# Another order of the steps between two expert layers, and a weight load issued behind the loop instead of in it

## The chip, the cores and the metric

The kernel runs on one core of a Trainium2 chip. Its engines are TensorE (PE: matmuls; PEld is its weight load, which overlaps), VectorE (DVE), ScalarE (ACT), GpSimd (POOL) and SyncE (SP). Each runs its own instructions in program order and waits for the others by semaphores; DMA transfers are issued from an engine's queue (here SP's, ACT's and POOL's) and move by themselves. The metric is the time of one execution on the device in microseconds (us); the lower the better.

## What is computed

Two layers on x, (4, 512, 512) f32 (2048 tokens of width 512), each an attention part and an expert part, gated by the tanh of a scalar:

```python
x = x + tanh(g_xattn[0]) * set_attention(layernorm(x), ctx)     # every token, 4 sets of 64
x = x + tanh(g_ffn[0])   * experts0(layernorm(x))               # 32 experts, top 6, at most 192 tokens each, + shared expert
x = x + tanh(g_xattn[1]) * causal_mha(layernorm(x), ctx, ctx)   # 16 heads, 64 keys
x = x + tanh(g_ffn[1])   * experts1(layernorm(x))               # 8 experts, top 2, inner width 352, + shared expert
```

Two facts of the reference matter for what follows. In the second attention the mask hides all 64 keys from every token but the last 64 of a batch; those others get the plain mean of the values, so the kernel computes that attention for the last row tile of each batch alone. And the shared expert of the last layer, `silu(x Wg + bg) * (x Wu + bu) Wd + bd` with inner width 704, needs no routing: it is computed in two halves (inner widths 320 and 384), the first of them between the two expert loops.

## The kernel before

**Tiles.** The 2048 tokens are 16 row tiles of 128 rows, x0 to x15, resident in SBUF. Tile t belongs to batch t // 4; a group g holds the tiles g, 4+g, 8+g, 12+g, one of each batch, so that group 3 has the last tile of every batch: 3, 7, 11, 15.

**The first expert loop** runs over pieces of experts, PE-bound, and writes weighted rows to y_dram. A token's sum over its experts is formed by fetches: one POOL indirect DMA (L1063) fetches, for one row tile, the k-th expert's row of each of its 128 tokens into a buffer `yk` (7 buffers, NYK), and one DVE addition puts it on the tile (L1104; L1106 for a tile's last one, which also leaves the row sums for the layer norm; then one ACT Square, L1057, gives the sum of squares). There are 76 fetches in all (six for tiles 0 to 8, fewer for the others). The string SUMS (L68) gives their order; the first 22 are asked for while the loop still runs, the other 54 behind it. At L1258 stands a branch on a count of tokens (not taken here), which every engine passes; POOL waits there for its outstanding fetches. I number the sums whose fetch is issued behind it s1 to s54; in front of s1 stand six more whose fetches were issued before it.

**The stage between the loops** is written out by hand. The string ORDER (L49) is a list of step names; in_steps (L671) calls them one after the other, and each call issues the next part of a generator. The engines' program order is exactly the order in which the parts issue. The steps:

- `s` (sums4): one addition (and Square), then the request for the next fetch.
- `e2`, `e3` (shared0): the first layer's shared expert on groups 2 and 3: two chunks of gate and up products on PE (L630, 16 matmul records each), Silu on ACT (L636), two DVE instructions that give `it0s` (L642, L643), then per tile the output product (PE L650, in one of two PSUM buffers `po0s`) and its addition on DVE (L657).
- `q` (query3): layer norm of group 3 on ACT (L1274), after a reciprocal root on DVE (L1121 and helpers). `a0`, `a1` (stage3): the attention for two batches each: transposes `ptq`, scores, softmax, output; it ends with additions on group 3's tiles and new Squares.
- `n0` to `n3` (norm4), `t0` to `t3` (turn_in4), `l0` to `l3` (logs): layer norm of a group (ACT L1133), its transposes (PE L282, ACT L283), the router's logits (PE L1146, L1152) and the choice of two experts (DVE L1159 to L1168).
- `d0` to `d3` (shared4): the first half of the last layer's shared expert on a group: PE L1361 (gate, up), ACT L1366, DVE L1367, PE L1377 and L1384, DVE L1387. Its weights are those that `k` loads first.
- `r0`, `r1` (route4): for half of the tokens (groups 0 and 1; then 3 and 2): positions on PE (L1175, L1176), some 40 DVE instructions that end with the table `ent` (L1209 to L1211), then 16 POOL indirect DMAs (L1216) that scatter the entries to slot_dram.
- `p` (plan4): a plan of expert tiles on DVE from the totals (PE L1419), then the request of the finished slot table from DRAM (POOL L1460, `tab`), a selection by matmul (PE L1464, `pslot`), and from it on DVE the row numbers `gat` and `put` by which the last expert loop gathers and scatters.
- `w` (first_weights): POOL gathers of two expert tiles' weights (L1396).
- `k` (loads): first call, on ACT's queue, load_shared4: gate and up weights (L782, 1.31 MB) and down weights (L783, 0.52 MB; L786, twice 0.13 MB) of the last layer's shared half; second call the keys and values of two batches (L1245, L1246, 1.5 MB).

Steps that stand in the ORDER ahead of PE's or ACT's arrival at the branch's far side may in the built program lie beside the loop's end on that engine: before, `k`'s first call is issued by ACT at 427 to 437 us, in the loop's last two pieces.

**Behind the stage**, from 641.6 us on, the last expert loop and the second half of the shared expert run, on PE almost without a gap.

```python
    while coming:          # sums4
        add4()
        ask4(NT2 - 1)
        yield
```

Of the kernel before, what the change touches and what calls it, by code (L numbers as in the profile page):

```python
# [46 lines left out]


ORDER = """  # L49
e3 s k s*2 e3*2 s*4 e3 e2 s*7 e2 s*2 e3 s*2 e3 s*2 e3 s*2 e3 s*4 e2 s e2 s q e2 n0 e2*2 n0 s*4 a0 a1 s*2 n0 t0  # L50
a0 n0 s n0 t0 s t0*2 a0 s e2 s*3 k s*3 l0 s d0 n1 d0 n1 s d0*2 n1 t1 l0 d0 l0 n1*2 a0 t1 s*2 d0 s t1 s a1 t1 a0
l1 s a1 a0 s*2 d1 s a1 l1*2 d0*2 a1 s*2 d1 a1 r0 s*2 n3*2 s n3 d1 r0 n3 s t3 s d1 t3 n3 n2 d0 r0 n2*3 r0 t3 r0
t3 n2 d1 d0 t2*2 l3 t2*2 d3 d1 d3 l2 r0 l3 l2 r0 l3 r0 l2 d1 r1 r0 d2 r1 p r1*3 d1 p d3 d2 r1 d1 d2 d3 d2*2 d1
r1 p r1 d2 p d2 d3 r1 d2 w p d3*2 p d3 p*2 w d3*2 d2 p d2
"""


# [8 lines left out]

NAHEAD = 22
SUMS = """  # L68
3 7 0 4 8 3 7 0 4 8 3 7 0 4 8 3 7 0 4 8 6 2 3 4 8 7 8 4 12 0 11 12 11 12 0 7 15 1 15 11 3 1 5 1 9 5 9 1 9 1 9 5
5 13 13 13 1 5 9 5 6 14 2 10 6 2 2 14 10 6 6 6 10 2 2 10  # L70
"""
NW = 3
NW0 = 4
# [1671 lines left out]
```

## Time and profile before

| | us |
|---|---|
| median of 3 runs | 1056.91 (1056.79 to 1057.18) |
| the profiled execution | 1056.65 |
| its span | 1054.9 |
| PE busy in it | 982.4 (93%) |
| DVE, POOL, ACT busy | 445.9, 380.5, 196.1 |
| the stage between the loops | 437.6 to 641.6 |

Times in the profile count from the span's start. An instruction's row in a timeline reads: start, duration, engine, line, operation, out<-in, tile sizes, how many were merged (x8), and in brackets the time its engine sat idle before it and what released it. A line "A <- B: 7.6, 1, 7.6" in the list of waits gives total, number and longest.

A few rows of waits in the stage (437 to 642 us):

```profile
POOL yk L1063 <- DVE x L1104: 16.7, 10, 5.7
DVE x L1104 <- DMA yk<-y_dram,rows_of: 11.8, 15, 2.6
PE po0s L650 <- DVE x L657: 7.6, 1, 7.6
DVE x L1106 <- DMA yk<-y_dram,rows_of: 6.3, 9, 2.2
PE po0s L650 <- DVE it0s L643: 3.2, 1, 3.2
DVE it L1367 <- ACT sg L1366: 3.0, 3, 1.9
```

and the loads of the shared half's weights on ACT's queue:

```profile
427.09 0.39 ACTq L782 DMA_DIRECT2D wall<-in_wsgu1a_dram  x1
429.69 0.49 ACT L870 ACTIVATE sgb<-g 128x384 f32<-128x384 f32 x1 [3.73 <-PE g L865]
435.87 0.39 ACTq L783 DMA_DIRECT2D wall<-in_wsd_dram  x1
436.29 1.17 ACTq L786 DMA_DIRECT2D wall<-in_wsd_dram  x2
```

### The profile page before, as it was taken

The page shows a single profiled execution, that of the slowest core. Times are in us where ns is not written, and L with a number is a line of the kernel's source. Part 1 is how long each engine was busy: PE and PEld are TensorE (multiplying, and loading weights), DVE is VectorE, ACT ScalarE, POOL GpSimd, SP SyncE. Part 2 cuts the span into 40 slices and gives each one's busy share as a digit, 9 for nine tenths or more (in the row PEclk, how much of TensorE's full clock was granted, in tenths as well). Part 3 has the DMA queues.
Part 4 walks back from the last instruction along what each step waited for, and adds up shares of the span by engine and source line. Part 5 has one row for each costly group of instructions (what it writes and reads, how often), then busy time and mean ns, then how long its engine had stood idle before and what let it go on. Part 6 is the DMA issues. An engine that isn't in the chain of part 4 may idle for free. (4 is left out here: it accounts for less than half of the span.)

```text
span 1054.9 us, 11755 instructions
## 1 busy us (share of the span) xinstructions
PE 982.4 (93%) x3762; PEld 578.3 (55%) x3762; DVE 445.9 (42%) x1218; ACT 196.1 (19%) x410; POOL 380.5 (36%) x420
## 2 busy tenths in 40 slices
PE   5568889999999999978999979999999999999998
PEld 2133348777878787634554434555555555544443
DVE  4878973323222322568885442122222222227111
ACT  1263111111111111015544002111111111100000
POOL 3001053353333333767623634445545445200000
PEclk8889989999999999989999989999999999999999
DMA  8722135798888799957722066247536535537111
GB/s 316 307 101 80 45 92 175 235 306 284 264 312 280 283 321 336 339 161 212 249 77 91 1 169 204 79 140 235 168 95 197 163 103 171 193 122 255 40 40 40
DMA packets 88671, 192.03 MB, mean 182 GB/s; under 512 B 24910, under 2 KB 42222, under 8 KB 82208
## 3 DMA queue, kind: packets, MB, share of 16 engines
q1 hardware_dynamic: 58800, 110.82, 29.4%
q0 software_dynamic: 28656, 76.76, 24.1%
q10 hardware_dynamic: 1152, 3.67, 1.0%
q8 instruction: 31, 0.51, 0.2%
q14 instruction: 32, 0.26, 0.1%
HBM read 206.16 MB, written 35.60 MB: 229 GB/s over the span
## 5 line engine op out<-in xcount | busy, mean ns | idle before, releaser
L1063 POOL DMA_INDIRECT yk<-y_dram,rows_of x76 | 84.4, 1111 | 50.4 <-DVE x L1104 18.4
L834 POOL DMA_INDIRECT xb<-h_dram,get x48 | 48.0, 1000 | 145.5 <-DVE get L830 71.0
L1586 PE MATMUL por<-wall,itr 128*128 128x512 f32 (+1 forms) x216 | 98.7, 592 | 0.0
L865 PEld LDWEIGHTS g<-lnT,wall 128*128 128x128 f32 x512 | 85.6, 194 | 21.4 <-issue 19.4
L1566 PE MATMUL pgr<-wall,xrT 128*128 128x352 f32 x288 | 91.7, 461 | 5.2 <-DMA wall<-in_wgu_dram,wrow 4.4
L865 PE MATMUL g<-lnT,wall 128*128 128x192 f32 x512 | 92.8, 336 | 1.4 <-ACT lnT L283 1.4
L1569 DVE SCALAR_TENSOR_TENSOR sgr<-pur,slots,sgr 128x352 f32<-128x352 f32 x36 | 21.0, 584 | 166.5 <-PE pur L1566 162.1
L1566 PE MATMUL pur<-wall,xrT 128*128 128x352 f32 x288 | 91.1, 459 | 0.0
L881 PE MATMUL pob<-wall,itb 128*128 128x512 f32 (+1 forms) x256 | 90.1, 599 | 0.0
L865 PE MATMUL u<-lnT,wall 128*128 128x192 f32 x512 | 88.4, 326 | 0.0
L865 PEld LDWEIGHTS u<-lnT,wall 128*128 128x128 f32 x512 | 84.1, 190 | 0.0
L1589 POOL DMA_INDIRECT y_dram<-yr,put x36 | 36.8, 1022 | 122.2 <-DVE yr L1588 121.9
L1361 PE MATMUL pg<-lnT,wall 128*128 128x512 f32 (+1 forms) x224 | 80.3, 536 | 0.1
L1361 PE MATMUL pu<-lnT,wall 128*128 128x512 f32 (+1 forms) x224 | 79.5, 531 | 0.0
L872 DVE TENSOR_TENSOR itb<-u,sgb 128x384 f32<-128x384 f32 x32 | 17.8, 558 | 136.8 <-PE u L865 130.4
L1566 PEld LDWEIGHTS pur<-wall,xrT 128*128 128x128 f32 x288 | 54.7, 190 | 30.5
L1566 PEld LDWEIGHTS pgr<-wall,xrT 128*128 128x128 f32 x288 | 51.9, 190 | 29.5 <-DVE yr L1588 3.6
L1586 PEld LDWEIGHTS por<-wall,itr 128*128 128x128 f32 (+1 forms) x216 | 41.0, 190 | 41.9 <-issue 34.9
L1377 PE MATMUL po<-wall,it 128*128 128x512 f32 x128 | 60.7, 608 | 0.8 <-DVE x L1387 0.8
L1361 PEld LDWEIGHTS pu<-lnT,wall 128*128 128x128 f32 (+1 forms) x224 | 35.0, 175 | 40.6 <-issue 37.5
L886 DVE TENSOR_SCALAR y<-pob,share 128x512 f32<-128x512 f32 x48 | 36.0, 750 | 48.4 <-PE pob L881 48.4
L1361 PEld LDWEIGHTS pg<-lnT,wall 128*128 128x128 f32 (+1 forms) x224 | 33.9, 175 | 40.8 <-issue 39.0
(413 smaller groups left out, 1291.6 us busy)
## 6 DMA issues: line engine op xcount, KB each, us to landing
wall<-in_wgu_dram SPq DMA_DIRECT2D x32, 1024.0 KB
wall<-in_wd_dram SPq DMA_DIRECT2D x32, 512.0 KB
y_dram<-y SPq DMA_DIRECT2D x32, 256.0 KB
q<-rp SPq DMA_DIRECT2D x256, 32.0 KB
y<-y_dram SPq DMA_DIRECT2D x32, 256.0 KB
lnT<-in_xT_dram SPq DMA_DIRECT2D x4, 1024.0 KB
x<-in_x_dram SPq DMA_DIRECT2D x16, 256.0 KB
h_dram<-h SPq DMA_DIRECT2D x16, 256.0 KB
```

The source lines that it names most:

```text
L834: G.indirect_dma_start(out=rows0[i], out_offset=None, in_=h_dram[:, :], in_offset=bass.IndirectOffsetOnAxis(ap=get2[:, i : i + 1], axis=0) ...
L865: PE.matmul(p_[:, ic, :], lhsT=weights[e][0][:, c, a * I0 + ic * P : a * I0 + (ic + 1) * P], rhs=x_[:, c, :], start=(c == 0), stop=(c == D ...
L872: V.tensor_tensor(its[e], two[1], sg, ALU.mult)
L881: PE.matmul(po[p_, :], lhsT=its[e][:, ic, at : at + n], rhs=weights[e][1][:, ic, :], start=(ic == 0), stop=(ic == I0 // P - 1),)
L886: V.tensor_scalar(y, po, share.pop(i), None, ALU.mult)
L1063: G.indirect_dma_start(out=yk, out_offset=None, in_=y_dram[:rows, :], in_offset=bass.IndirectOffsetOnAxis(ap=rows_of[:, t, k : k + 1], axi ...
L1361: PE.matmul(p_[m, :n], lhsT=wgu[:, a, c, i], rhs=lnT[g][:, c, k], start=(c == 0), stop=(c == DC - 1))
L1377: PE.matmul(po, lhsT=it[:, ic, k * P : (k + 1) * P], rhs=wd[:, ic, :] if ic < 2 else wd2, start=(ic == 0), stop=(ic == 2),)
L1566: PE.matmul(p_, lhsT=xbT[:, c, :], rhs=wgu[:, a, c, :], start=(c == 0), stop=(c == DC - 1))
L1569: V.scalar_tensor_tensor(sg[:, :I1], pu, slots[:, 1, i : i + 1], sg[:, :I1], ALU.mult, ALU.mult)
L1586: PE.matmul(po, lhsT=it[:ni, ic, :], rhs=wd[:ni, ic, :], start=(ic == 0), stop=(ic == 2))
L1589: d = G.indirect_dma_start(out=y4_dram[:, :], out_offset=bass.IndirectOffsetOnAxis(ap=put4[:, i : i + 1], axis=0), in_=yr, in_offset=None, ...
```

## The change

Only the two strings change. The steps and the sums are the same, each as often as before; their order differs. The first `k` moves from the third place of ORDER to behind the sum s12, and so, in the built program, on ACT from the loop's end to a place behind the Square of tile 12. `e3` goes first as a whole and then `e2`, where before their parts alternated; sums of a tile stand closer to each other in another order; in the second half the shared half's parts (`d`) and the routing (`r`, `p`) are woven in another way.

```diff
 ORDER = """
-e3 s k s*2 e3*2 s*4 e3 e2 s*7 e2 s*2 e3 s*2 e3 s*2 e3 s*2 e3 s*4 e2 s e2 s q e2 n0 e2*2 n0 s*4 a0 a1 s*2 n0 t0
-a0 n0 s n0 t0 s t0*2 a0 s e2 s*3 k s*3 l0 s d0 n1 d0 n1 s d0*2 n1 t1 l0 d0 l0 n1*2 a0 t1 s*2 d0 s t1 s a1 t1 a0
-l1 s a1 a0 s*2 d1 s a1 l1*2 d0*2 a1 s*2 d1 a1 r0 s*2 n3*2 s n3 d1 r0 n3 s t3 s d1 t3 n3 n2 d0 r0 n2*3 r0 t3 r0
-t3 n2 d1 d0 t2*2 l3 t2*2 d3 d1 d3 l2 r0 l3 l2 r0 l3 r0 l2 d1 r1 r0 d2 r1 p r1*3 d1 p d3 d2 r1 d1 d2 d3 d2*2 d1
-r1 p r1 d2 p d2 d3 r1 d2 w p d3*2 p d3 p*2 w d3*2 d2 p d2
+s e3 s*4 e3*2 s*4 e3 s*3 e3 s*2 e3 s e3 s*3 k e3 s*3 e2 s e2 s*2 q s*3 e2 s*2 n0 a0 e2 a1 s n0 s a0 n0 s n0 t0 s
+e2 t0 s n0 e2 t0 s t0 a0 s*2 k s*3 e2 s d0 s*2 d0 s l0 s e2 d0 s n1 l0*2 n1 s d0 n1*2 d0 s n1 t1*2 a0 t1 s t1 d0
+a1 a0 a1 l1 a0 d1 s*2 l1 s a1 l1 s d1 d0 a1 d0 s*2 a1 s*2 n3*3 d1 s*3 r0 n2 t3 d1 t3 n3 r0*2 d0*2 n2 t3 r0*2 n2
+r0 n3 r0 t2 d1*2 t2 t3 n2 d1 n2 t2*2 l3 l2 l3*2 l2 d3 l2 p r1 r0 d2 d3 r1*2 d3 r1*2 d1 p d2 d1 r0 p d2 d1 d3 r1
+p d3 p r1*2 d3 d2 r1 w d3 d2 p d3 d2*3 p*3 d3*2 d2*2 w
 """
 SUMS = """
-3 7 0 4 8 3 7 0 4 8 3 7 0 4 8 3 7 0 4 8 6 2 3 4 8 7 8 4 12 0 11 12 11 12 0 7 15 1 15 11 3 1 5 1 9 5 9 1 9 1 9 5
-5 13 13 13 1 5 9 5 6 14 2 10 6 2 2 14 10 6 6 6 10 2 2 10
+3 7 0 4 8 3 7 0 4 8 3 7 0 4 8 3 7 0 4 8 6 2 8 4 1 12 3 12 5 11 9 7 7 12 3 11 11 15 15 4 8 2 0 0 9 5 13 1 5 13 5
+9 9 9 1 13 1 1 5 5 1 10 6 14 6 10 6 2 6 14 2 10 10 2 2 6
 """
```

## The prediction

> **What bounds the kernel now.** I read first the busy times of each engine by stage (columns: start and end, length, busy us of PE, PEld, DVE, ACT and POOL with instruction counts, granted PE clock, DMA share, GB/s). The run has a span of 1054.9 us.
>
> ```profile
> 461.80:491.60 29.80, 19.00 (x37) 7.95 (x38) 22.41 (x64) 10.73 (x23) 23.33 (x22) 0.83 0.70 187
> ...
> 580.10:623.00 42.90, 42.85 (x156) 19.34 (x154) 22.21 (x90) 3.01 (x5) 25.09 (x26) 1.00 0.21 11
> 623.00:629.20 6.20, 0.01 (x1) 0.04 (x1) 1.39 (x2) 0.00 (x0) 2.19 (x3) 0.73 0.94 393
> 629.20:641.60 12.40, 11.56 (x28) 4.79 (x28) 2.22 (x6) 0.62 (x1) 4.99 (x5) 0.86 0.62 224
> 641.60:1054.90 413.30, 402.99 (x1206) 216.82 (x1204) 108.69 (x169) 47.94 (x127) 136.30 (x135) 1.00 0.43 140
> ```
>
> From 641.6 on PE is busy for 403.0 of 413.3 us, and the change touches nothing there. The stage before it ends with PE idle at 623 to 629.2. What ends that wait stands in POOL's timeline:
>
> ```profile
> 453.18 1.07 POOL L1063 DMA_INDIRECT yk<-y_dram,rows_of  x1 [4.13 <-DVE x L1104]
> ...
> 565.98 1.03 POOL L1216 DMA_INDIRECT slot_dram<-ent,slot  x1 [27.54 <-DVE a L1209]
> ...
> 589.72 0.98 POOL L1216 DMA_INDIRECT slot_dram<-ent,slot  x1 [0.30 <-DVE plan L1424]
> ...
> 611.61 0.98 POOL L1216 DMA_INDIRECT slot_dram<-ent,slot  x1 [0.30 <-issue]
> ...
> 622.57 0.60 POOL L1460 DMA_DIRECT2D tab<-slot_dram  x1 [7.30 <-DMA slot_dram<-ent,slot]
> ```
>
> and in PE's:
>
> ```profile
> 469.36 5.13 PE L650 MATMUL po0s<-wall,it0s 128*128 128x512 f32 x8 [7.57 <-DVE x L657]
> ...
> 485.45 6.26 PE L650 MATMUL po0s<-wall,it0s 128*128 128x512 f32 x10 [3.24 <-DVE it0s L643]
> ...
> 500.87 3.70 PE L1361 MATMUL pg<-lnT,wall 128*128 128x512 f32 x8
> ...
> 629.19 1.04 PE L1464 MATMUL pslot<-pick,tab 128*128 128x39 f32 x4 [6.24 <-DMA tab<-slot_dram]
> ```
>
> So the end hangs on one train: DVE makes the first routing table (step r0), POOL starts its 32 scatters at 565.98, the last has landed when the table is asked back at 622.57, and pslot starts at 629.19. First scatter to pslot is 63.2 us, pslot to the end 425.7. A change of order shows in the time through three clocks: (1) the first scatter; (2) the second table, whose scatters begin at 589.72 (DVE writes it at 588.59 + 0.22 = 588.81, 0.9 us of cover); (3) PE's arrival at pslot, 622.95, with 6.24 us of cover. PE's early idle, 7.57 + 3.24, is paid out of that cover: it is not on the path.
>
> **The change, part by part.** Sums, fetches, scatters and matmuls keep their number. In the built programs PE has the same set of work ahead of pslot and the same behind it, and POOL the same 32 scatters, table request and weight gathers behind the fetches. What moves is who stands ahead of whom.
>
> *Front of PE.* Before, PE has 6 products of L630 after 437.59, then outputs; after, only e3's four stand ahead of its outputs. They end at 437.59 + 4 × 3.43 = 451.3. Their second product is limited on DVE (L642, L643) behind the sums s1 and s2, the first two fetched behind the branch:
>
> ```profile
> 453.59 0.55 DVE L643 TENSOR_SCALAR it0s<-it0s,lim 128x512 f32<-128x512 f32 x1
> 456.73 0.69 DVE L1104 TENSOR_TENSOR x<-x,yk 128x512 f32<-128x512 f32 x1 [2.60 <-DMA yk<-y_dram,rows_of]
> 458.11 0.69 DVE L1104 TENSOR_TENSOR x<-x,yk 128x512 f32<-128x512 f32 x1 [0.68 <-DMA yk<-y_dram,rows_of]
> ```
>
> 458.11 + 0.69 + 0.74 + 0.55 = 460.1 less overlap: it0s is ready at 460.0, PE idle 8.7 (was 7.57). The half-clock window that follows costs what it did (5.13 for x8 against 3.60 elsewhere: 1.5). Then 16 output matmuls (2 × 3.45) and the other four products (13.7): 460.0 + 6.9 + 1.5 + 13.7 = 482.1, where before had the same work done at 481.2. Next stand the transposes of q: q needs the sum s17, at 456.73 + 16 × 1.41 (POOL's pace: 1.11 a fetch and 0.30 between) = 479.3, its add 0.7, Square 0.9, the reciprocal root (11 small DVE instructions, 2.1 where a later norm has them, at 557.60 to 559.74) and ACT's first q 0.7: 483.7, so PE idles 1.6 to 2. The other half waits for ACT copies behind two more Squares: 2 to 3 idle. d0 starts near 500.5 (500.87) but still owes one output of group 2 and the logits product (1.88 + 1.07). So PE is 2.3 to 2.9 late there, and gives back idles of 1.0 and 0.2 later: it reaches pslot near 624.2, 5 us ahead of the table. Cost: nothing while that cover stands; if it were gone, 1.2.
>
> The Trainium skill weighs against this front: "TensorE: Matmul & The Clock Gate", "Why this matters for your kernels", wants no PE gap over about 3 us, since one idle window halves the clock. The row agrees (clock 0.83, 5.13 for 3.60). By the rule the 8.7 us gap would be a loss of some 1.5 more; by the rows before pays it too, at 7.57, and pslot's cover hides either.
>
> *DVE up to the first scatter.* From the first L642 to the table DVE is busy 93.07 of 117.40 us. Named waits: sums for fetches 7.6 and 6.3, L1367 for ACT 3.0, L1387 for PE 1.4, L1121 0.9, L1159 0.2. After: the 5.5 of the last four vanish; new are two L657 behind late outputs of group 2 (1.8 of matmuls less 0.7 of DVE's own, 1.1 each), one logits wait (row elsewhere 1.16: 1.2) and two L1121 at 0.9: 5.2. The L642/L643 pair moved behind the 2.60 wait, where it ran free: +1.3. Two sums fewer and one L1387 more ahead of the table: −1.4 + 0.7. Sum +0.3, with −1.9 to +2 for what I may have placed wrong (a new wait that isn't there, or one more of the size of L1367's longest, 1.9).
>
> *The load.* L782, L783 and L786 (2.10 MB) leave the loop for ACT's queue behind the Square of s12, tile 12: 456.73 + 11 × 1.41 + 0.69 + 0.9 = 473.8. Four issues of ~0.45 hold ACT about 1.8 (the four of L1245/L1246 took that); behind them stands the Silu of e3 or e2, idle then. Needed by d0 near 500: 393 GB/s in the window at 623 against 187 in that at 461.8 leave 200 beside the fetches, by which 2.10 MB takes 10.5 and lands by 485. But it runs beside the fetches s13 to s21, which q waits for. Landing times of the fetches, at 453:489 and at 505:517 (beside the 1.5 MB of L1245/L1246):
>
> ```profile
> DMA to landing us min/median/max: 3.8/3.8/3.9
> ```
> ```profile
> DMA to landing us min/median/max: 7.2/7.2/7.2
> ```
>
> So a price of 0 to 3.4 once: seven buffers at 1.41 hold 9.9 us of pace, so a longer landing delays the stream but doesn't slow it. The nearest row is 505:517, where DVE lost 2.4 in two waits. A DVE that comes 2.4 later spends less in its own new waits: half of 2.2 and of 1.2 is 1.7. I take 0.7. What the loop gains (its fetches landed in 4.5 to 5.0) is no gain at PE, which is full there to 451.
>
> The skill's page "DMA: Bandwidth & Descriptors", "Issuing engines are not separate DMA queues", says that DMAs of any issuer interleave on the same 16 engines; by it ACT's queue shields nothing and the full 3.4 is due, time 1060.4.
>
> *Second table.* pos of r1 moves with PE, 580.1 to about 581.4; table at 588.8 + 1.3 = 590.1, 17th scatter slot at 589.72 + 1.0 = 590.7: not in the way.
>
> **Sum.** 0.3 + 0.7 = +1.0 at the first scatter (567.0), carried whole to pslot (630.2) and the end: 1056.65 + 1.0 = 1057.65 for the profiled kind of run, whose own time lies 0.26 below the median 1056.91. Forecast 1057.7.
>
> **Rivals.** (A) Slower: the load hits the fetches that q and the early norms wait for, and nothing gives it back: 0.3 + 2.4 to 3.4, middle +3.2, 1059.9. For it: 7.2 against 3.8. Against: DVE's queue has other work between sums. It decides once the first scatter comes after 568.1. (B) Faster: the 5.5 of old waits go and the new 5.2 don't arise, no contention: 0.3 − 5.2 = −4.9, of which clock 2 lets through 0.9 if the second table stays and all if it follows DVE; middle −2.9, 1053.8. For it: that table waits on PE for 5.30 and 1.16 of its way, so an earlier PE frees it. Against: PE is later, not earlier. (C) The request for tab before four steps of shared work instead of one hides pslot's 6.24: 1050.5. Against: PE's set ahead of pslot is unchanged, so there is nothing to hide it with; under 0.02, counted with B. (D) Weights miss d0: needs 15 us more than worked out; counted with A.
>
> **How the numbers follow.** A measurement here tells about 0.2%, 2.1 us, from no change. Chances: the forecast (1054.8 to 1059.0) 0.48; A 0.32; B 0.20. The likeliest one's own range is 1055.6 to 1059.0. Range for 8 in 10: down to B's middle, less a little for its lower half, 1053.9; up to A's full price 1060.4 plus 0.4: 1060.8.
>
> **What would show it.** First scatter near 567.0 (A: past 568.1; B: before 564); pslot's wait about 5 to 6, still on the table; PE idle near 8.7 before the first po0s, now named it0s L643; landings of the fetches issued at 470 to 485 above 3.8; d0 within 1 us of 500.9. Wrong if pslot's wait is gone (PE late), if the second train's first scatter waits for DVE, or if the stretch behind 641.6 changes length.

## The result and the profile after

The changed kernel is slower: 1063.04 us (median of 7 runs, 1061.6 to 1064.28) against 1057.87 for the kernel before (7 runs: the three shown ahead of the prediction and four more, 1057.87 to 1060.78). The ratio of the means is 1.0044 (95% interval 1.003 to 1.0059), about 4.7 us; against the four further runs alone the means differ by 3.7. Its profiled execution took 1061.60, span 1059.9, against 1056.65 and 1054.9. The likeliest case, no change at 1057.7, was wrong, and the range ended at 1060.8.

POOL's timeline of the changed kernel, at the places shown of before:

```profile
454.28 1.00 POOL L1063 DMA_INDIRECT yk<-y_dram,rows_of  x1 [4.38 <-DVE x L1104]
...
569.39 1.03 POOL L1216 DMA_INDIRECT slot_dram<-ent,slot  x1 [22.76 <-DVE a L1209]
...
594.58 0.98 POOL L1216 DMA_INDIRECT slot_dram<-ent,slot  x1 [0.30 <-DVE plan L1424]
...
616.17 0.98 POOL L1216 DMA_INDIRECT slot_dram<-ent,slot  x1 [0.30 <-issue]
...
627.37 0.60 POOL L1460 DMA_DIRECT2D tab<-slot_dram  x1 [7.54 <-DMA slot_dram<-ent,slot]
```

The first scatter, 565.98 before, starts at 569.39. That is past the point (568.1) that the prediction named for the slower rival. The loop itself ended 0.70 later in this execution (first L630 on PE at 438.29, 437.59 before), so that the stage up to the first scatter is 2.7 us longer: 131.1 against 128.4. From there to pslot it is 64.3 (63.2), from pslot to the end 426.2 (425.7). The sum, 0.7 + 2.7 + 1.1 + 0.5, is the 5.0 between the spans. Of these only the 2.7 can be laid to the change: the distance from first scatter to pslot was 69.5 in a later execution of the kernel before, so that 1.1 is nothing there. One pair of traces does not prove the 2.7 either, since the stage up to the first scatter varies by more between executions of one kernel (table below); the waits that follow and the times of the experiments have to carry it.

PE's timeline shows where PE stands still ahead of that:

```profile
461.02 8.78 PE L650 MATMUL po0s<-wall,it0s 128*128 128x512 f32 x14 [7.98 <-DVE it0s L643]
...
488.00 1.97 PE L282 MATMUL ptq<-ident,q 128*128 128x128 f32 x8 [4.46 <-ACT q L1274]
491.78 1.97 PE L282 MATMUL ptq<-ident,q 128*128 128x128 f32 x8 [1.82 <-ACT qT L283]
...
504.08 3.60 PE L1361 MATMUL pg<-lnT,wall 128*128 128x512 f32 x8
...
633.72 1.07 PE L1464 MATMUL pslot<-pick,tab 128*128 128x39 f32 x4 [6.33 <-DMA tab<-slot_dram]
```

PE's first idle is 7.98 and is named it0s L643, 0.4 longer than the 7.57 that before had. pslot's wait is 6.33, on the table still, so PE's own delays did not decide. What is new is 4.46 us before the transposes of q. Behind it stand the load, on ACT's queue, and DVE; below are the load's first rows, DVE's timeline, and the time to landing of the fetches issued from 470 to 480:

```profile
473.48 0.39 ACTq L782 DMA_DIRECT2D wall<-in_wsgu1a_dram  x1
473.96 0.39 ACTq L783 DMA_DIRECT2D wall<-in_wsd_dram  x1
```
```profile
457.75 0.69 DVE L1104 TENSOR_TENSOR x<-x,yk 128x512 f32<-128x512 f32 x1 [4.29 <-DMA yk<-y_dram,rows_of]
...
478.75 0.69 DVE L1106 SCALAR_TENSOR_TENSOR x<-x,yk 128x512 f32<-128x512 f32 x1 [3.38 <-DMA yk<-y_dram,rows_of]
...
481.06 0.69 DVE L1104 TENSOR_TENSOR x<-x,yk 128x512 f32<-128x512 f32 x1 [1.42 <-DMA yk<-y_dram,rows_of]
```
```profile
DMA to landing us min/median/max: 6.3/7.1/7.8
```

The load leaves at 473.48, the fetches issued from 470 to 480 need 7.1 us to land instead of 3.9, and DVE stands still for 3.38 and 1.42 ahead of the additions at 478.75 and 481.06. The row by engine of these ten us, of before and then of the changed kernel (last two columns: the share of the time in which the DMA engines are busy, and GB/s), shows what the load does there:

```profile
474.00:484.00 10.00, 8.21 (x20) 3.31 (x18) 6.87 (x18) 3.74 (x9) 7.87 (x8) 1.00 0.68 188
474.00:484.00 10.00, 9.54 (x23) 3.93 (x21) 5.05 (x14) 2.32 (x7) 7.87 (x8) 1.00 1.00 350
```

POOL issues the same eight fetches in both, but with the load the DMA engines have no idle time left. The waits of DVE as a list, from the first L642 to the first table (449.9 to 569.9; total, number, longest):

```profile
DVE x L1104 <- DMA yk<-y_dram,rows_of: 11.5, 10, 4.3
DVE x L1106 <- DMA yk<-y_dram,rows_of: 6.0, 3, 3.4
DVE x L657 <- PE po0s L650: 3.0, 2, 2.1
DVE va_d L1121 <- ACT sq L1057: 1.8, 2, 0.9
DVE x L1387 <- PE po L1384: 0.8, 1, 0.8
```

Fetches cost DVE 17.5 us against 13.9 before; the other waits 5.6 against 5.5; its work 92.0 against 93.1. The difference is in the first number.

### The profile page after: what moved, and what is told of

It reads as the page before. It is cut to its first block, busy times and chain, and to the rows that moved or that the text cites. A ratio compares the mean times of both kernels' runs of the same rounds, so it can differ in the third digit from the quotient of the medians.

```text
span 1059.9 us, 11757 instructions
## 1 busy us (share of the span) xinstructions
PE 987.6 (93%) x3762; PEld 582.8 (55%) x3762; DVE 445.6 (42%) x1218; ACT 195.9 (18%) x410; POOL 378.5 (36%) x420
```

## The experiments

The theories, as the expectations number them: 1, the load beside the fetches makes DVE late; 2, the second half's weave costs; 3, the order of sums and of e3/e2 costs by itself; 4, the load costs wherever it lies behind the loop; 5, not the bytes but the four issues on ACT's queue. The runs were made on several chips, on which the kernel before had medians of 1063.5 to 1068.8, so only ratios to the kernel before on the same chip are compared. Some traces hold waits that nothing in the program explains; the trace names them "remote" or "issue". "First scatter" is its distance from the first L630 on PE, which is the loop's end; each is from one trace, and the four traces of before lie 5.1 apart, so that it supports a time and does not replace it.

| kernel | first scatter, us | ratio to before (95%) |
|---|---|---|
| before: first trace, b0, b1, b2 | 128.4, 132.7, 127.6, 130.4 | 1 (b0 to b2: 0.9984, 1.0003, 0.9998) |
| changed: first trace, a0 | 131.1, 131.3 | 1.0044 (1.003 to 1.0059), 1.0051 (1.0021 to 1.0081) |
| e3, e3b: changed, load in the loop | 127.0, 128.3 | 1.0012 (0.9996 to 1.0028), 0.9993 (0.9977 to 1.0008) |
| e6, e6b: e3 and four small DMAs | 134.1, 129.6 | 1.0046 (1.0019 to 1.0072), 1.0009 (0.9995 to 1.0023) |
| e7: changed, down weights alone late | 131.4 | 1.0024 (1.0011 to 1.0037) |
| e4: before, load late | 138.9 | 1.0058 (1.0036 to 1.008) |
| e5: changed, load just ahead of q | 132.5 | 1.0049 (1.0022 to 1.0076) |
| e9: changed, load ahead of the branch | 137.7 | 1.0095 (1.006 to 1.013) |
| e2, e2b: before's front, changed second half | 125.1, 128.0 | 1.001 (0.9995 to 1.0025), 0.9997 (0.9968 to 1.0026) |
| e1, e1b: changed front, before's second half | 134.9, 134.1 | 1.0041 (1.0025 to 1.0057), 1.0039 (1.0016 to 1.0063) |
| e8, e8b: e1 with the load in the loop | 136.6, 132.5 | 1.0043 (1.0018 to 1.0068), 1.0052 (1.0028 to 1.0077) |

**e3 and e3b: the load put back.**

```diff
-s e3 s*4 e3*2 s*4 e3 s*3 e3 s*2 e3 s e3 s*3 k e3 s*3 e2 s e2 s*2 q s*3 e2 s*2 n0 a0 e2 a1 s n0 s a0 n0 s n0 t0 s
+s e3 k s*4 e3*2 s*4 e3 s*3 e3 s*2 e3 s e3 s*3 e3 s*3 e2 s e2 s*2 q s*3 e2 s*2 n0 a0 e2 a1 s n0 s a0 n0 s n0 t0 s
```

> The changed kernel with the first k alone put back to the head of the order, so that ACT issues the 2.10 MB in the loop as before. Theory 1: fetch landings at 470 to 480 back to 3.6 to 4.5, DVE's waits for fetches in the front down by 3 to 3.6, first scatter at 566 to 567 and the time within 2 us of before (ratio 1.000 to 1.002). Theory 3 (the order of sums and of e3/e2 costs by itself, the load little): still 3 us or more above before.

> The changed kernel with the first k back in the loop, again, to narrow its interval (1.0012, 0.9996 to 1.0028 so far). Theory 1: 1.000 to 1.002, no fetch wait of DVE over 2 between 470 and 485, ptq waits for q 1.2 and not 4.5. Theory 3 (order of sums by itself): 1.003 or more.

The slowdown is gone: both intervals hold 1, and neither reaches 1.003. Landings at 470 to 480 in e3, and its PE at q:

```profile
DMA to landing us min/median/max: 3.6/3.6/3.6
```
```profile
485.61 1.37 PE L282 MATMUL ptq<-ident,q 128*128 128x128 f32 x8 [1.15 <-ACT q L1274]
```

Theory 1 holds, theory 3 falls for this second half of the order (for the other see e8): with the same order of sums, PE waits 1.15 for q instead of 4.46, and the first scatter is 2.8 to 4.3 us earlier than in the changed kernel's two traces. In e3 the DMA engines are busy for 0.63 of 474 to 484, at 187 GB/s.

**e4: the load alone moved, in the order of before.**

```diff
-e3 s k s*2 e3*2 s*4 e3 e2 s*7 e2 s*2 e3 s*2 e3 s*2 e3 s*2 e3 s*4 e2 s e2 s q e2 n0 e2*2 n0 s*4 a0 a1 s*2 n0 t0
+e3 s*3 e3*2 s*4 e3 e2 s*7 e2 s*2 e3 s*2 k e3 s*2 e3 s*2 e3 s*4 e2 s e2 s q e2 n0 e2*2 n0 s*4 a0 a1 s*2 n0 t0
```

> The kernel before with the first k alone moved behind the sum s12, as in the changed kernel, all else as before. Theory 1: fetches beside the load land in 6 to 8, first scatter 2.5 to 3.5 later, time 3 to 4 us above before (ratio 1.0028 to 1.004). Theory 3: within 1 us of before.

Slower by 0.58%, more than expected; DVE's timeline and the landings at 470 to 480:

```profile
481.17 0.69 DVE L1104 TENSOR_TENSOR x<-x,yk 128x512 f32<-128x512 f32 x1 [2.93 <-DMA yk<-y_dram,rows_of]
483.33 0.69 DVE L1104 TENSOR_TENSOR x<-x,yk 128x512 f32<-128x512 f32 x1 [1.47 <-DMA yk<-y_dram,rows_of]
```
```profile
DMA to landing us min/median/max: 6.8/7.1/7.5
```

The same signature, 4.4 us in two waits, without anything else of the change. The load is enough to make the kernel slower, and here too the DMA engines are busy without a break (1.00 at 357 GB/s, 478 to 486). Why it costs more here than in the changed order was not taken apart.

**e6, e6b and e7: issues or bytes.** e6 leaves the load in the loop and puts a step `z` behind s12; e7 issues L782 in the loop and L783 and L786 behind s12 (its lines stand 3 lower in the file). Parts of the two edits:

```diff
+    def tiny():
+        few = between.tile([P, 4, 8], F32, name="few")
+        for c in range(4):
+            A.dma_start(out=few[:, c, :], in_=wsd1[:P, 8 * c : 8 * c + 8])
+        yield
```
```diff
-        load_shared4(0, W4, A)
+        load_shared4(0, W4, A, "up")
+        yield
+        load_shared4(0, W4, A, "down")
         yield
```

> The changed kernel with the first k back in the loop and, in its place behind s12, four small DMAs on ACT's queue (4 KB each, to a tile that nothing reads). Theory 1 (bytes beside bytes): as with k in the loop, ratio 1.000 to 1.002, fetch landings at 470 to 480 near 4. Theory 5 (four issues that hold ACT about 1.7 us, so that the Squares of group 3 and q come later): ratio 1.003 to 1.005 and the landings near 4 all the same.

> As before: first k back in the loop, four small DMAs on ACT's queue behind s12. In the last call a wait of 7.2 us on nothing in the program lay in its trace and its time said 1.0046 with a wide interval. Theory 1 (bytes): within 0.001 of the kernel with k in the loop, in the same call. Theory 5 (issues hold ACT): 0.002 or more above it, with q late.

> The changed kernel with only the down weights (0.79 of the 2.10 MB, three of the four DMAs) issued behind s12, the gate and up weights in the loop. Theory 1, by bytes: a bit over a third of the load's price, DVE's fetch waits at 470 to 485 about 1 to 1.5 more than with k in the loop, time 1 to 1.5 us above it. Theory 5: nearly all of the price, 2.5 to 3.5.

The times do not separate issues from bytes. e6's 1.0046, taken alone, speaks for theory 5 (its trace holds a wait of DVE of 7.2 us that nothing in the program explains); e6b is 0.0016 above e3b and e7 another 0.0015, each with an interval that overlaps the one below it, and e7's 3.3 us above e3b lie where its expectation had theory 5. The traces do separate them. DVE's waits for fetches of over 0.7 between 475 and 485, e6b first, then e7:

```profile
479.48 0.69 DVE L1106 SCALAR_TENSOR_TENSOR x<-x,yk 128x512 f32<-128x512 f32 x1 [0.88 <-DMA yk<-y_dram,rows_of]
```
```profile
478.92 0.69 DVE L1109 SCALAR_TENSOR_TENSOR x<-x,yk 128x512 f32<-128x512 f32 x1 [1.59 <-DMA yk<-y_dram,rows_of]
...
482.35 0.69 DVE L1107 TENSOR_TENSOR x<-x,yk 128x512 f32<-128x512 f32 x1 [2.54 <-DMA yk<-y_dram,rows_of]
```

Four issues without bytes leave 0.9 us, as e3b has without them (0.78), with landings of 3.7 to 4.2 in e6b; PE's wait for q is 1.14 in e6 and 1.82 in e6b. The 0.79 MB of e7 bring 4.1, nearly the 4.8 of the whole 2.10 MB, with landings of 4.4 to 6.6 (median 5.5), and PE waits 3.94 for q. So at DVE it is the bytes, but not in proportion: theory 1 is right in kind, and its "a bit over a third" was wrong. The smaller load, too, leaves the DMA engines no idle time (share 1.0 at 478 to 484). In time e7 lies between e3b and the changed kernel, about half of the price; what share of it the issues have is not shown.

**e5 and e9: other places for the load.** e5 moves `k` from behind s12 to just ahead of `q`, e9 to between the two Silus of e3.

```diff
-s e3 s*4 e3*2 s*4 e3 s*3 e3 s*2 e3 s e3 s*3 k e3 s*3 e2 s e2 s*2 q s*3 e2 s*2 n0 a0 e2 a1 s n0 s a0 n0 s n0 t0 s
+s e3 s*4 e3*2 s*4 e3 s*3 e3 s*2 e3 s e3 s*3 e3 s*3 e2 s e2 s*2 k q s*3 e2 s*2 n0 a0 e2 a1 s n0 s a0 n0 s n0 t0 s
```
```diff
-s e3 s*4 e3*2 s*4 e3 s*3 e3 s*2 e3 s e3 s*3 k e3 s*3 e2 s e2 s*2 q s*3 e2 s*2 n0 a0 e2 a1 s n0 s a0 n0 s n0 t0 s
+s e3 s*4 e3*2 k s*4 e3 s*3 e3 s*2 e3 s e3 s*3 e3 s*3 e2 s e2 s*2 q s*3 e2 s*2 n0 a0 e2 a1 s n0 s a0 n0 s n0 t0 s
```

> The changed kernel with the first k moved only from behind s12 to just ahead of q, that is behind the fetches that q waits for. There DVE has other work and its fetches have landed ahead of it (no fetch wait of DVE between 484 and 515 in the changed kernel). Theory 1 (the load costs what DVE then waits for fetches): fetches issued at 486 to 497 land in 6 to 8 instead of 4 to 5, but DVE's waits for fetches fall by 3 or more, the first scatter comes 2 to 4 earlier than in the changed kernel, ratio 1.000 to 1.002. Theory 4 (the load costs wherever it lies behind the loop): no better than the changed kernel, 1.004.

> The changed kernel with the first k between the first and the second Silu of e3, so that ACT issues it at about 442 to 443, behind the loop's end, when POOL is about to wait for its outstanding fetches at the branch. If the load costs one longer landing of the fetches that somebody waits for, wherever it lies behind the loop: the fetches issued at 440 to 449 land in 6 to 8, the first fetch behind the branch comes 2 to 3 later than 454.3, the first scatter as late as in the changed kernel (131), ratio 1.003 to 1.005. If the gap at the branch takes it: 127 to 128.5, ratio 1.000 to 1.002.

In both places the load was no cheaper, so theory 1's expectation for e5 failed and theory 4 holds for them. e5's DVE, behind q now, with ACT and PE behind it, and e9's POOL at the branch:

```profile
493.96 0.69 DVE L1104 TENSOR_TENSOR x<-x,yk 128x512 f32<-128x512 f32 x1 [3.00 <-DMA yk<-y_dram,rows_of]
496.05 0.72 DVE L1106 SCALAR_TENSOR_TENSOR x<-x,yk 128x512 f32<-128x512 f32 x1 [1.40 <-DMA yk<-y_dram,rows_of]
```
```profile
497.06 0.72 ACT L1057 ACTIVATE sq<-x,st 128x512 f32<-128x512 f32 x1 [2.79 <-DVE st L1055]
```
```profile
498.18 1.97 PE L282 MATMUL ptq<-ident,q 128*128 128x128 f32 x8 [4.86 <-issue]
```
```profile
463.24 0.99 POOL L1063 DMA_INDIRECT yk<-y_dram,rows_of  x1 [8.46 <-DVE x L1104]
```

In e5 the wait ahead of q (3.83 in a0) is gone and 4.4 us appear behind it, where the changed kernel had none. It is not absorbed there: the Square of the late sum (497.06) stands in ACT's order ahead of the copies of q's transposes, and PE stands still for 4.86 until then. (The trace names no releaser for PE; that it is this chain is read from the order of the rows.) In e9 POOL waits at the branch, 8.46 instead of 4.38. The row names DVE's additions; they stand behind fetches that the load has slowed, and POOL's last semaphore of the branch (L1258) falls at 461.8, when the DMA engines have just run empty (18 GB/s at 461 to 462, 0 behind it). So the whole stream starts 4.3 us later behind the loop's end (20.3, in the changed kernel 16.0). e9 has the highest time, 0.95%, more than either of its expectations; not all of it need be the load's, since it rests on six runs and in its trace PE stands still on nothing in the program for 1.40 and 2.92 at 508 and 512, and for 8.6 at 627 to 637.

**e1, e2, e8: halves of the order.** Behind the 102nd step both orders have done the same set of steps and the same 65 sums, so that they can be joined there. In short, with AFTER and BEFORE for the two lists of steps:

```diff
-ORDER = BEFORE
+ORDER = AFTER[:102] + BEFORE[102:]     # e1, sums cut at 65; e8 with its first k at the head
+ORDER = BEFORE[:102] + AFTER[102:]     # e2
```

> The order and sums of the changed kernel up to its 102nd step (behind the second a0 of batch pair 0, where both orders have executed the same set of steps and sums), then the rest of the order of before. Theory 1 (the load beside the fetches makes DVE late, all in the front): fetches issued at 470 to 480 land in 6 to 8 us, the first scatter comes 2.5 to 3.5 later than in the kernel before, and the time is 3 to 5 us above it (ratio 1.003 to 1.005), nearly as slow as the changed kernel. Theory 2 (the second half's weave, with later layer-norm stores beside the scatters, is what costs): within 1.5 us of before.

> The reverse: before's order and sums up to the same 102nd step, then the rest of the changed order. The weights load stays in the loop. Theory 1: within 1.5 us of before (ratio 0.9985 to 1.0015), landings of the fetches at 470 to 480 near 3.8. Theory 2: 2 to 5 us above before, with a scatter train (first to last of 32) 1 us or more longer than 45.6.

> Before's order up to the 102nd step, then the changed order, again. In its first trace the first scatter came 125.1 us behind the loop's end, against 127.6 to 128.4 in the kernel before. If the second weave gains 2.5 to 3 us there and it reaches the end: ratio 0.997 to 0.998. If it is given back behind the first scatter: 0.999 to 1.001, with the second train's first scatter, the last landing or PE's arrival later by as much, seen beside the trace of before of this call.

> The changed order up to the 102nd step with the first k in the loop, then before's order: the fourth cell. If front, weave and load add up at the first scatter: front plus 2 to 3, so loop's end to first scatter 130 to 131.5, ratio 1.001 to 1.003. If the front costs nothing: 127.5 to 128.5 and 1.000.

> The fourth cell again (changed front with the load in the loop, then before's order): its first trace had two waits of ACT of 3.4 and 3.9 us at 491 to 499 that belong to nothing in the program, and DVE's wait of 6.8 behind them. Without such waits: loop's end to first scatter 130 to 131.5, ratio 1.001 to 1.003. If they are there again, they belong to this order: 135 or more, 1.004.

> The changed front with its load behind s12, then before's order, again, on the same chip as e8b: loop's end to first scatter 3 to 4 more than e8b without foreign waits, ratio 1.003 to 1.006 and 0.002 to 0.004 above e8b, if the load costs the same under either second half.

e2 is as fast as before, and so are e3 and e3b with the same second half: theory 2 falls. Of e2's gain of about 3 us at the first scatter, seen in its first trace, the second left none that can be told from before's 127.6 to 132.7, and neither time shows it. e1 is as slow as the changed kernel, but does not show that the load is the reason, because of e8, which stays open. Under before's second half, the load in the loop did not make the time better (1.0043 and 1.0052 against 1.0041 and 1.0039), though e1b was expected 0.002 to 0.004 above e8b. e8's trace holds two waits of ACT on nothing in the program,

```profile
494.73 0.37 ACT L283 COPY qT<-ptq 128x256 f32<-128x256 f32 x1 [3.40 <-remote]
498.95 0.37 ACT L283 COPY qT<-ptq 128x256 f32<-128x256 f32 x1 [3.85 <-remote]
```

and e8b's has five of PE at 619 to 628, 6.2 us together, of which b0, the kernel before itself, shows four. The order cannot be cleared of such waits, since they came in both traces of it, but they came in different places, and neither trace shows what the order costs without them. So the load's price is shown for the orders of before and of the change as they stand, not for every order; and that the changed front costs nothing by itself (theory 3) is shown only with the changed second half.

**b0 and a0: both kernels again on another chip.**

> The kernel before, unchanged, profiled on the chip of this call, so that the others of the call can be laid beside its trace: ratio 1.000 within 0.001. From the loop's end (first L630 on PE) to the first scatter near 128.4 us as in its first trace; the train from the first scatter to pslot is 63.2 us if it belongs to the kernel, 66 to 68 if it belongs to the chip of the call, as the four kernels of the last call had it.

> The changed kernel, unchanged, on the same chip: ratio 1.003 to 1.006. From the loop's end to the first scatter 2.5 to 4 us more than in the kernel before of this call; the train to pslot the same within 1.5 us.

The ratio came again; the two expectations on the traces failed. a0's first scatter is 131.3 behind the loop's end, 1.4 less than b0's 132.7 and not 2.5 to 4 more, and its train to pslot is 78.4 against 72.2. Both traces hold foreign waits: in b0 PE stands still on nothing in the program for 2.33 at 506 and for 8.4 at 622 to 630; in a0 a wait of DVE of 23.87, named remote, ends at 628.45 and holds PE for 12.83. PE's cover at pslot was gone in both (pslot came 14.05 behind the table's request in a0; its wait was 0.32 in b0, the kernel before). The train from the first scatter to pslot belongs to the execution, not to the kernel: 69.5 in b1, 65.7 in b2, 72.2 in b0.

## Why the prediction was wrong

- **What bounds the kernel** held: the end moved with the first scatter, pslot still waited for the table (6.33), and from pslot to the end it took 426.2 (425.7 before).
- **Front of PE** held in kind: idle 8.7 forecast and 7.98 measured, from it0s L643, hidden by pslot's cover. The half clock came again (0.50 in the row below, third column from the end). It cost more than the 1.5 of the sum: 14 output matmuls took 8.78, and 6.3 at the rate of 8 in 3.60. At the end it cost nothing, pslot's wait being 6.33. The sign "d0 within 1 us of 500.9" failed: d0 began at 504.08, late by PE's wait for q.

```profile
458.00:466.00 8.00, 4.97 (x6) 2.18 (x7) 5.61 (x9) 0.00 (x0) 6.29 (x6) 0.50 0.67 188
```

- **DVE's exchanged waits** held in their total, in part by luck: 5.2 new ones forecast, 5.6 measured, but L657 took 3.0 instead of 2.2, the wait for the logits of 1.2 did not come, and L1387's, taken as gone, kept 0.8; the first wait behind the branch 4.29, the forecast 2.60 + 1.3 being 3.9.
- **The load** is the step that failed, in its size: 0.7 in the sum. The issue (473.8 forecast, 473.48 measured) and the fetches that it hits were right, and the upper bound of 3.4 was near what was paid. I took 0.7, by giving 1.7 back because "a DVE that comes 2.4 later spends less in its own new waits". It gives nothing back: q comes later with DVE, PE waits for q (4.46 instead of 1.15 to 1.54 with the load in the loop), and so the outputs for which DVE waits in L657 come later as well (these waits are 3.0 with the load, 3.0 and 1.3 in e3 and e3b). Nor did 200 GB/s stay free beside the fetches without harm to them: the DMA engines were busy for the whole of 474 to 484, at 350 GB/s. Measured: 4.8 in two waits, 3.6 more in all fetch waits than before, 2.8 to 4.3 at the first scatter between e3 or e3b and the two traces of the changed kernel. That is less than or about the 3.7 to 4.7 of the times; where a rest would lie is not shown.
- "A longer landing delays the stream but doesn't slow it" was right, and is why the price is paid once and in full: until s20 or so DVE adds as fast as POOL issues, later DVE itself is the limit (no wait of it for a fetch from 484 to 515). That neither has room to catch up is argued from these rows, not tested.
- The slower rival A named this mechanism, its place and its point of decision; its price, 3.2, lies within the 2.8 to 4.3 at the first scatter. The Trainium skill's page "DMA: Bandwidth & Descriptors", section "Issuing engines are not separate DMA queues", spoke for it, and this case agrees: ACT's queue shielded nothing (landings of 7.1 instead of 3.9). The measured median is above A's 1059.9 in part because the kernel before itself came out at 1057.87 in the runs compared.
- The gain at the loop, taken as nothing, was nothing: e3 has the load in the loop and is no slower for it.

## What to carry to other kernels

In this kernel a bulk load moved beside a paced stream of small fetches cost about what it added to the landing of one fetch (3.2), once and in full, where the consumer had no slack; a bit over a third of the bytes brought most of the consumer's waits and about half of the time. Before giving a delay back to later waits, ask whether the work that one then waits for hangs on the same late result. Of the places tried the load was cheapest where the bound engine had its operands already, in the loop, and dearest just ahead of the branch at which POOL waits for its outstanding fetches. Whether there is room for a load shows in the DMA engines' share over the very stretch of the load, not over the stage.

## What the runs showed that I had not expected

- The wait at the branch grows with the landing of the last fetches: 4.38 us without the load, 8.46 with 2.10 MB issued ahead of it.
- Over the stretch from 461 to 504 the DMA engines are busy for 0.80 at 251 GB/s, as if there were room; in the ten us of the load they have none (1.00 at 350 GB/s), and that is where the fetches land in 7.1 us instead of 3.9.
- From the first scatter to the request of the table the unchanged kernel took 56.6 us in its first trace and 59.0 to 65.5 in three later ones (b2, b1, b0): more than the whole difference at stake, which is why one pair of traces could not have settled it.
